# A reordered start, split products and masks on another engine in a two-layer kernel

## The chip, the cores and the metric

The kernel runs on one core of one Trainium2 chip, in one launch. The metric is the device time in microseconds (us); lower is better. The engines are TensorE (PE in the profile; its weight loads are PEld), VectorE (DVE), ScalarE (ACT), GpSimd (POOL) and SyncE (SP, which issues most DMAs). Each engine takes its instructions in the order in which they were put on its queue.

## The reference, cut to what matters

Everything is float32. The input x is (2, 1024, 512), so 2048 rows of 512. Two layers, each on a normalized copy of x:

```python
xn = _layernorm(x)
x = x + L0_attn(xn) + L0_ffn(xn)
xn = _layernorm(x)
x = x + L1_attn(xn) + L1_ffn(xn)
```

- `L0_attn` is a small branch: layer norm, a projection to 8 ranks, a linear recurrence over the 1024 rows, a projection back, and a small MLP of rank 8.
- `L0_ffn` is `fwht(silu(x @ W1.T) * (x @ W3.T)) @ W2.T` with 2048 hidden columns; `fwht` is the Walsh-Hadamard transform of the hidden row.
- `L1_attn` is causal softmax attention with 16 heads of 32, with a biased projection before it and after it.
- `L1_ffn` is `silu(x @ w_gate) * (x @ w_up)`, of each four neighbours the two largest in magnitude kept, times `w_down`.

## The kernel before, in words

**Blocks and pools.** The 2048 rows are four blocks of 512 (`TT`). `x1[i]` holds block i as four tiles of 128 rows, `xt0[i]` and `xt1[i]` hold its normalized transpose for layer 0 and layer 1. All stages are one program; three memory pools follow one another: `a` (layer 0), `b` (attention), `c` (the second feed-forward). PSUM is used as three double banks (`wide0` to `wide2`) and two single banks.

**Order.** `in_program_order` ties every instruction of PE, DVE, ACT and POOL to the one before it on its engine, in the order in which the Python code emits them. So an instruction that waits holds up everything behind it on its engine. Small work is put between the large products by hand: `put0(n, at, f, ...)` (layer 0) and `put1` (layer 1) queue a function for unit n at one of seven places, and `hook(at)` calls it there; `put0(0, 10, ...)` means unit 1, place 3.

**Gate and up products, `gate_up`, L186.** One unit is 128 columns of the hidden width for a pair of blocks (x, y). Its eight 512-wide block products are made with seven, by Winograd's scheme: `products` (L175) makes one block product, 4 matmuls, which are 8 PE records of the profile (3.43 us). The order in a unit is: `w1,x` into bank pair pa; copy to `e[0]` (L208, ACT); `s0,t0` into pc; `s1,t1` added into pa; copy to `e[1]` (L216, ACT); `other_half` into a third pair pb, added to `e[0]` on DVE (L204), then hook 3; `s2,t2` added into pa; copy to `e[2]` (L222, ACT); `e[2]` plus pc on DVE (L224); `w2,t3` added into pa; `s3,y` added into pc; `e[1]` plus pc (L234). A product that adds into pa waits until the ACT copy of pa is done; the last into pc waits until L224 has read pc. The sums `t0` to `t3` of the inputs are made by `combine_x` (L148, four DVE subtractions of 128x1024), the sums `s0` to `s3` of the weights by `combine_w` (L165, four POOL operations). Where `first` is given (unit 0 of either layer), `other_half` comes right after the copy to `e[0]`. There are 16 units in each layer: units 0 to 7 are blocks 0 and 1, units 8 to 15 blocks 2 and 3.

**The start.** `load_x` brings the tiles of block 0. `ln_stats(i, half)` makes the statistics of two tiles on DVE (L113, L114, L106) and their reciprocal deviation on POOL (L107). `ln_scale` makes the offsets on DVE (L119) and the normalized tiles z: on ACT for block 0 (L123), on DVE for block 1 (L537). `ln_turn` transposes z on PE (L132) and copies it out on ACT (L136). `ln_turn(1, 1)`, the last one, is called in `begin`, which also makes `t0` and `t1`; so the first product of the sums follows it directly. `branch_in` (L579) is 32 thin products (24 columns out) for each half of a block. `prepare` (four POOL operations) and `prepare_last` (thin products, L489 to L505) make constants of the branch.

**The transform.** The Walsh-Hadamard transform is applied to W2. `fwht_rows(q)` (L424) multiplies quarter q by a Hadamard matrix in four products, each evicted by ACT (L431); before unit 3 these use the two single banks in turn. Four `fwht_step` on DVE (L442, L443; two operations of 128x1024 each) follow, the last of them into `w2h`, from which POOL makes the sums of the down weights (L741 onward). The down products (L297) start in unit 3; the second of them waits for `hidden_first` and `hidden_last` (L265 to L273, four DVE operations).

**Attention.** The steps of `first` (row maxima) run 13 steps (`ahead`) before those of `second`, 96 steps in all, 12 for each of 8 units. A step of `second` makes scores (L1095, L1101), exponentials on ACT (L1112) into `pt`, for the diagonal block a mask on POOL (`affine_select`, L1117), then in the next step `gather` multiplies by the values (`o`, L1137) and adds `pt` into the running sum `acc` (L1145): on POOL, or on DVE once the row maxima are over. At its end stands the out-projection (`po`, L990), then layer 1's feed-forward.

**The end.** Layer 1's last group is multiplied by its down weights row block by row block (`row_down`, L1449): 4 matmuls of 512 columns, an addition on DVE (L1459), a store of 256 KB (L1462).

Of the kernel before, what the change touches and what calls it, by code (L numbers as in the profile page):

```python
# [35 lines left out]
def two_layers(ctx: ExitStack, tc: tile.TileContext, t: dict, out: bass.AP):  # L36
# [137 lines left out]

    def products(pair, a, x, start=False, stop=False):  # L175

        for m in range(2):
            for k in range(2):
                nc.tensor.matmul(  # L179
                    pair[:, m, :], a[:, m, k, :], x[:, k, :],  # L180
                    start=start and k == 0, stop=stop and k == 1, skip_group_check=True,
                )

    turns = 0

    def gate_up(pool, name, w1, w2, s, x, y, tt, h, hook, first=None):  # L186

# [12 lines left out]

        def other_half():
            pb = ps_pair(f"p1_{name}", turns % 3)
            products(pb, w1[:, :, 2:, :], x[:, 2:, :], start=True, stop=True)
            nc.vector.tensor_add(e[0], e[0], pb)  # L204
            hook(3)

# [11 lines left out]
        if not first:  # L218
            other_half()
        products(pa, s[2], tt[2])  # L220

        nc.scalar.copy(e[2], pa)  # L222
        silu(0, 0, e[0][:, 0, :])
        nc.vector.tensor_add(e[2], e[2], pc)  # L224
# [119 lines left out]
    with tc.tile_pool(name="a", bufs=1) as a:  # L344
# [78 lines left out]

        def fwht_rows(q):  # L424

            tags = ("x1_2", "x1_3") if q % 2 else ("xt_2", "xt_3")
            w2x[q] = [res.tile([P, NC, P], F32, tag=tag, name=f"w2{tag}_{q}") for tag in tags]
            for c in range(0, NC, 4):
                bank = one_bank(f"pw_{q}_{c}")
                nc.tensor.matmul(bank, had, w2h[:, q, c : c + 4, :], start=True, stop=True)  # L430
                nc.scalar.activation(  # L431
                    w2x[q][0][:, c : c + 4, :].rearrange("p c d -> p (c d)"), bank,
                    AF.Copy, scale=1.0 / math.sqrt(HID),
                )
# [83 lines left out]
        def ln_stats(i, half):  # L518
            js = slice(2 * half, 2 * half + 2)
            statistics(mv0[i][:, js], rs0[i][:, js], x1[i][:, js, :], 2, f"a{i}_{half}")  # L520

        zs = {}

        def z_tile(name, tag="z"):
            return a.tile([P, 2, D], F32, tag=tag, name=name)

        def ln_scale(i, half, tag="z"):


            js = slice(2 * half, 2 * half + 2)  # L530
            offsets(nm0[i][:, js], mv0[i][:, js], rs0[i][:, js])
            zs[i, half] = z_tile(f"z0_{i}_{half}", tag)
            for m in range(2):
                j = 2 * half + m
                d, x = zs[i, half][:, m, :], x1[i][:, j, :]
                if i == 1:
                    nc.vector.tensor_scalar(  # L537
                        d, x, mv0[i][:, j, 0:1], rs0[i][:, j : j + 1], ALU.subtract, ALU.mult
                    )
                else:  # L540
                    scaled(d, x, nm0[i], rs0[i], j)

        def ln_turn(i, half):
# [239 lines left out]
        for half in range(2):  # L783
            put0(0, 3, branch_in, 0, half)
            put0(0, (1, 2)[half], branch_in, 1, half)
        for q, n in enumerate(((0, 2), (0, 4), (1, 2), (1, 4))):
            put0(*n, fwht_rows, q)
            for m in range(4):
                n, at = (0, (4, 5, 6, 6)[m]) if q == 0 else divmod(4 * q + 3 + m, 7)
                put0(n, at, fwht_step, q, m)  # L790
        put0(0, 6, prepare)
        put0(2, 6, load_x, 2)
# [35 lines left out]

        for k in ((0, 0), (0, 1)):
            ln_stats(*k)  # L830
        ln_scale(0, 0)
        ln_turn(0, 0)
        ln_stats(1, 0)
        ln_scale(0, 1, "e2")
        ln_turn(0, 1)
        ln_stats(1, 1)
# [3 lines left out]
        def begin():  # L840
            nonlocal tt
            ln_turn(1, 1)
            tt, make_first, second = combine_x(a, xt0[0], xt0[1], "a0")
# [16 lines left out]
        for n in range(2 * NU):  # L860
# [7 lines left out]
            def hook(at):  # L868
# [11 lines left out]
                a, f"a{n}", *weights_of[n], xt0[i0], xt0.get(i0 + 1), tt,  # L880
                lambda m, i: h[:, 2 * (n % 2) + m, i, :], hook, begin if n == 0 else None,
            )
            for m in (2 * n + 4, 2 * n + 5):
# [19 lines left out]


    first_gu = {}
    with tc.tile_pool(name="b", bufs=1, reuse_waits="tile") as b:

# [15 lines left out]
            out=mask, in_=mask, compare_op=ALU.is_ge, fill=MASKED,  # L923
            base=0, pattern=[[-1, P]], channel_multiplier=1,
        )
        identb = b.tile([P, P], BF16, name="identb")
# [147 lines left out]
        def shift_rows(u, half):  # L1074
# [9 lines left out]
            nc.vector.tensor_copy(negs[u, half], px[:, :NJ].rearrange("p t c -> p (t c)"))  # L1084

        def weights(u, j, kt):

# [18 lines left out]
            for p in range(2):  # L1106
# [7 lines left out]
                )  # L1114
                if kt >= 4 * j:
                    d = pt[:, :, s : s + P]
                    nc.gpsimd.affine_select(  # L1117
# [5 lines left out]

        held, sums = {}, {}

        def gather(u, j, kt, s, pts):

            bb, hg = units[u]
            if kt == 0:
                held[u, j] = ps_bank(f"o_{u}_{j}", 0)  # L1130
                sums[u, j] = pts
            po = held[u, j]
# [8 lines left out]
            if kt:  # L1141

                eng = nc.vector if per * u + 4 * j + kt + ahead >= len(second) else nc.gpsimd
                for acc, pt in zip(sums[u, j], pts):
                    eng.tensor_add(acc[:, :, s:], acc[:, :, s:], pt[:, :, s:])  # L1145
# [6 lines left out]
        def total(u, j):  # L1152

            pw = ps_wide(f"w_{u}_{j}")[:, 0, :]
            for h in range(4):
                rows = slice(h * HD, (h + 1) * HD)
                nc.tensor.matmul(  # L1157
                    pw[rows, :], ones, sums[u, j][h // 2][:, h % 2, :],
                    start=True, stop=True, tile_position=(0, h * HD),
# [162 lines left out]
        for m in range(QT, QT + NJ):  # L1322
            rest.append((n, n + 9, project_out(m)))
        while rest or open_parts or fixed:
            one_part(n)
            what_is_fixed(n)
            n += 1
# [8 lines left out]
    with tc.tile_pool(name="c", bufs=1, reuse_waits="tile") as c_:  # L1336
# [112 lines left out]
        def row_down(n, i, j):  # L1449

            block = 2 * units[2 * n][0] + i
            bank = ps_wide(f"dr_{n}_{i}_{j}")[:, 0, :]
            for r in range(4):
                nc.tensor.matmul(  # L1454
                    bank, hs[n][:, r, i, j * P : (j + 1) * P], wd[n][:, r, :],
                    start=(r == 0), stop=(r == 3),
                )
            x = x1[block][:, j, :]
            nc.vector.tensor_add(x, x, bank)  # L1459
            if n % G == G - 1:  # L1460
                row = block * TT + j * P
                nc.sync.dma_start(out=out[row : row + P, :], in_=x)  # L1462

# [51 lines left out]

        tt, next_tt, second = None, None, None
        s_of = {}
# [4 lines left out]
        for n, (pb, g, half) in enumerate(units):  # L1522
# [12 lines left out]
            def hook(at):  # L1535
                nonlocal tt, next_tt, second
                if n == at == 0:
                    tt, *make = combine_x(c_, x, y, "c0")
                    for f in make:
                        f()  # L1540
                for f, *args in between1.pop((n, at), ()):
# [5 lines left out]
                if at == 5 and n == len(units) // 2 - 1:  # L1547
                    next_tt, first, second = combine_x(c_, xt1[2], xt1[3], "c1")
                    first()

            gate_up(
                c_, f"c{n}", gu_w.pop((n, 0)), gu_w.pop((n, 1)), s_of.pop(n), x, y, tt,
                lambda m, i: h[:, 2 * half + m, i, :], hook,
                (lambda: (y, tt)) if n == 0 else None,
            )
# [79 lines left out]
```

## Time and profile before

| | |
|---|---|
| median of 3 runs | 1847.09 us (1846.87, 1847.09, 1848.96) |
| the profiled execution, its own time | 1850.59 us |
| its span, first to last instruction | 1848.8 us |
| mean granted TensorE clock | 0.994 |
| PE busy | 1798.2 us, 97% |
| DVE, POOL, ACT busy | 1127.4 us (61%), 821.1 us (44%), 478.5 us (26%) |
| DMA | 68.12 MB, mean 37 GB/s |

A timeline line gives start, duration, engine, line of the kernel, operation, tiles and shapes, and in square brackets the idle time before it and what ended it. Lines merge neighbours of one kind; a matmul in float32 counts as two records. A line of the waits gives who waited for whom, the total in us, how often, and the longest. A line of the stretches (windows) gives the busy time and number of instructions of PE, PEld, DVE, ACT and POOL, then the granted clock (PEclk), the DMA share and GB/s. Before the first record of the clock (20.7 us) the PEclk column shows 1.00 whatever it was; there the durations tell it.

### The profile page before, as it was taken

Reading aid. Unit: us, or ns where it says so; the run is one execution under the profiler, and the core shown is the slowest. Engines: PE = TensorE matmul, PEld = TensorE weight load, DVE = VectorE, ACT = ScalarE, POOL = GpSimd, SP = SyncE. Lnnn points to the kernel's source line nnn. Section 1 sums busy time; section 2 is a strip of 40 time slices with the busy share of each in tenths; the row PEclk is TensorE's granted clock in tenths of the full one; section 3 lists DMA queues with packets and bytes.
Section 4 is the critical chain, followed back from the end, with each engine's and each line's share of the span. In section 5 each row is a group of like instructions: output and inputs, shape, how many; then the busy total and the mean of one; then the engine's idle time right before and its main releaser. Section 6 shows DMA issues by size and latency. Waiting matters only on the chain.

```text
span 1848.8 us, 18896 instructions
## 1 busy us (share of the span) xinstructions
PE 1798.2 (97%) x7348; PEld 918.6 (50%) x7348; DVE 1127.4 (61%) x1464; ACT 478.5 (26%) x683; POOL 821.1 (44%) x711
## 2 busy tenths in 40 slices
PE   6999999999999999999999999999999999999999
PEld 4446565655655564333333333333455555555544
DVE  3685444565543438565657656642768678768665
ACT  2322222122221102334333443412211221212120
POOL 4335364246552222467667756732244244343410
PEclk9999999999999999999999999999999999999999
DMA  6121111011101100000001000011101101211101
GB/s 228 35 80 34 35 35 38 31 46 35 35 23 34 35 7 23 1 12 12 13 1 35 12 12 1 24 46 34 35 23 57 57 23 58 91 35 46 46 1 46
DMA packets 29465, 68.12 MB, mean 37 GB/s; under 512 B 3392, under 2 KB 11584, under 8 KB 27840
## 3 DMA queue, kind: packets, MB, share of 16 engines
q1 hardware_dynamic: 28656, 66.61, 10.9%
q8 instruction: 59, 0.97, 0.2%
q10 hardware_dynamic: 720, 0.30, 0.1%
q14 instruction: 30, 0.25, 0.0%
HBM read 62.70 MB, written 4.19 MB: 36 GB/s over the span
## 4 chain that ended last, share of the span: by engine, by line
PE 88%; DVE 5%; POOL 2%; ACT 2%; issue 2%; DMA 1%; ACTq 0%; POOLq 0%; DVEq 0%
PE p_a L179 20%; PE p_c L179 19%; PE d L297 19%; PE pq L990 6%; PE m L1042 4%; PE s L1095 4%; PE o L1137 3%; PE po L990 3%; PE pv L990 3%; PE dr L1454 2%; POOL acc L1145 2%; PE w L1157 1%; DVE tops L1050 1%; PE pp L579 1%; PE s L1101 1%
## 5 line engine op out<-in xcount | busy, mean ns | idle before, releaser
L315 POOL TENSOR_TENSOR x<-x,de 128x512 f32<-128x512 f32 x87 | 125.9, 1462 | 298.4 <-DVE x L310 163.7
L1145 POOL TENSOR_TENSOR acc<-acc,pt 128x1024 f32<-128x1024 f32 (+3 forms) x138 | 233.7, 1719 | 0.0
L1050 DVE TENSOR_REDUCE tops<-m 128x2 f32<-128x1024 f32 (+2 forms) x192 | 180.8, 956 | 49.1 <-PE m L1042 44.7
L310 DVE TENSOR_TENSOR x<-x,d 128x512 f32<-128x512 f32 x145 | 99.3, 685 | 149.8 <-PE d L297 148.6
L1112 ACT ACTIVATE pt<-s 128x1024 f32<-128x1024 f32 (+3 forms) x160 | 115.1, 766 | 180.3 <-PE s L1101 167.1
L297 PE MATMUL d<-td,h 128*128 128x256 f32 x592 | 139.9, 380 | 2.2 <-DVE h L272 2.2
L297 PEld LDWEIGHTS d<-td,h 128*128 128x128 f32 x592 | 112.2, 190 | 46.2 <-issue 29.0
L990 PE MATMUL pq<-xt,wqk 128*128 128x512 f32 x256 | 125.1, 617 | 0.8 <-ACT qk L1006 0.8
L179 PE MATMUL p_a<-t_a,s_a 128*128 128x512 f32 x256 | 119.2, 610 | 2.1 <-DVE t_a L156 2.1
L179 PE MATMUL p_a<-xt,w 128*128 128x512 f32 x256 | 117.7, 603 | 0.7 <-ACT xt L136 0.7
L179 PE MATMUL p_c<-xt,s_c 128*128 128x512 f32 x256 | 115.2, 593 | 2.5 <-DVE e_c L224 1.4
L179 PE MATMUL p_a<-xt,s_a 128*128 128x512 f32 x256 | 116.6, 598 | 0.0
L179 PE MATMUL p_c<-xt,gu 128*128 128x512 f32 x256 | 114.9, 592 | 0.0
L179 PE MATMUL p_c<-t_c,s_c 128*128 128x512 f32 x256 | 114.6, 592 | 0.0
L1049 DVE TENSOR_TENSOR m<-m,mask 128x256 f32<-128x256 f32 x128 | 54.7, 427 | 98.2 <-PE m L1042 93.7
L1042 PE MATMUL m<-qk,qk 32*128 32x512 f32 (+3 forms) x768 | 107.7, 536 | 3.6 <-ACT acc L1112 3.0
L1095 PE MATMUL s<-qk,qk 32*128 32x512 f32 (+3 forms) x768 | 93.8, 532 | 3.7 <-ACT pt L1112 2.3
L172 POOL TENSOR_TENSOR s_c<-gu,s_c 128x512 f32<-128x512 f32 x16 | 20.4, 1275 | 135.9 <-PE p_c L179 135.9
L1117 POOL TENSOR_SCALAR_AFFINE_SELECT pt<-pt 128x256 f32<-128x256 f32 x112 | 48.4, 448 | 71.2 <-ACT pt L1112 70.6
L990 PEld LDWEIGHTS pq<-xt,wqk 128*128 128x128 f32 x256 | 44.5, 191 | 66.5 <-issue 62.1
L179 PEld LDWEIGHTS p_a<-xt,s_a 128*128 128x128 f32 x256 | 47.2, 190 | 57.1 <-issue 56.7
L179 PEld LDWEIGHTS p_c<-xt,s_c 128*128 128x128 f32 x256 | 48.5, 190 | 54.2 <-issue 52.9
(240 smaller groups left out, 3049.2 us busy)
## 6 DMA issues: line engine op xcount, KB each, us to landing
w<-in_W SPq DMA_DIRECT2D x32, 512.0 KB, 3.6
gu<-in_gu SPq DMA_DIRECT2D x32, 512.0 KB, 3.6
wd<-in_down SPq DMA_DIRECT2D x8, 1024.0 KB, 4.8
x<-in_x SPq DMA_DIRECT2D x16, 256.0 KB, 4.2
w2h<-in_W2q SPq DMA_DIRECT2D x4, 1024.0 KB, 11.7
xr<-in_x SPq DMA_DIRECT2D x16, 256.0 KB, 2.7
wqk<-in_WqkvT SPq DMA_DIRECT2D x16, 256.0 KB, 3.2
out_x<-x SPq DMA_DIRECT2D x16, 256.0 KB, 2.0
```

The source lines that it names most:

```text
L179: nc.tensor.matmul(pair[:, m, :], a[:, m, k, :], x[:, k, :], start=start and k == 0, stop=stop and k == 1, skip_group_check=True,)
L297: nc.tensor.matmul(out_[:, j, :], lhs[:, q, j * P : (j + 1) * P], rhs[:, q], start=m in (0, 1, 3, 4) and j == q == 0, stop=j == q == 1, sk ...
L310: nc.vector.tensor_add(r, r, out_)
L315: nc.gpsimd.tensor_add(r, r, u2[half])
L990: nc.tensor.matmul(got[0], lhs(k), rhs(k), start=(k == 0), stop=(k == KC - 1))
L1042: nc.tensor.matmul(pair[h // 2][:, h % 2, :e], q[rows, qt * P : (qt + 1) * P], k[rows, c * 512 : c * 512 + e], start=True, stop=True,)
L1049: nc.vector.tensor_add(d, d, mask.unsqueeze(1).to_broadcast([P, 2, P]))
L1050: nc.vector.tensor_reduce(out=tops[u][:, c, qt, 2 * p : 2 * p + 2], in_=pair[p][:, :, :e], axis=mybir.AxisListType.X, op=ALU.max,)
L1095: nc.tensor.matmul(pair[h // 2][:, h % 2, s:], k[rows, kt * P : (kt + 1) * P], q[rows, cols], start=True, stop=False,)
L1112: nc.scalar.activation(pt[:, :, s:], pair[p][:, :, s:], AF.Exp, scale=1.0 / math.sqrt(HD))
L1137: nc.tensor.matmul(po[rows, s:], v[:, rows], pts[h // 2][:, h % 2, s:], start=(kt == 0), stop=last, tile_position=(0, h * HD),)
L1145: eng.tensor_add(acc[:, :, s:], acc[:, :, s:], pt[:, :, s:])
```

## The change

1. **Start.** Before anything else PE makes 8 products of the identity with itself (`keep_awake`), then 4 and 3 with parts of x tiles 1 and 3; nobody reads their bank. The statistics of tiles 2 and 3 are split (`tile_stats`) around the scaling of the first half; the second half of block 0 is scaled on DVE, its offsets after it; all that comes ahead of block 1's statistics.
2. **Block 1's last transposes** move from `begin` to hook 3 of unit 0, between the two `branch_in` of block 0. `prepare` moves from hook 6 to hook 1 of unit 0.
3. **The transform's rows** come two products at a time, in eight hooks instead of four; the first quarter's steps come one hook later.
4. **`split`** in `gate_up`: `other_half` is cut in two, one half before `s2,t2` and one after it, with the addition L204 and hook 3 behind the second. It is used in unit 2 of layer 0 and in units 0, 1 and 14 of layer 1; unit 0 of layer 1 no longer uses `first`.
5. **Attention.** In the last unit the masks are minima with `allowed` on DVE, instead of `affine_select` on POOL; in exchange the running sums of its first half stay on POOL.
6. **Layer 1's first input sums** are made during the out-projection after attention, in a pool `sums` of their own.
7. **The very last `row_down`** goes in two column halves, each with its own addition and store.

```diff
-    def products(pair, a, x, start=False, stop=False):
+    def products(pair, a, x, start=False, stop=False, of=(0, 1)):
-        for m in range(2):
+        for m in of:
...
-        def other_half():
-            pb = ps_pair(f"p1_{name}", turns % 3)
-            products(pb, w1[:, :, 2:, :], x[:, 2:, :], start=True, stop=True)
-            nc.vector.tensor_add(e[0], e[0], pb)
-            hook(3)
+        def other_half(of=(0, 1)):
+            nonlocal pb
+            if 0 in of:
+                pb = ps_pair(f"p1_{name}", turns % 3)
+            products(pb, w1[:, :, 2:, :], x[:, 2:, :], start=True, stop=True, of=of)
+            if 1 in of:
+                nc.vector.tensor_add(e[0], e[0], pb)
+                hook(3)
...
         if not first:
-            other_half()
+            other_half((0,) if split else (0, 1))
         products(pa, s[2], tt[2])
         nc.scalar.copy(e[2], pa)
+        if split:
+            other_half((1,))
         silu(0, 0, e[0][:, 0, :])
         nc.vector.tensor_add(e[2], e[2], pc)
...
-        def fwht_rows(q):
+        def fwht_rows(q, half):
...
-            for c in range(0, NC, 4):
+            for c in range(NC // 2 * half, NC // 2 * (half + 1), 4):
...
+        def tile_stats(i, j):
+            st = sm.tile([P, 4, 6], F32, tag="st", name=f"st_a{i}_{j}")
+            nc.vector.bn_stats(st[:, 0, :], x1[i][:, j, :])
+            nc.vector.bn_aggr(mv0[i][:, j, :], st[:, 0, :])
...
             put0(0, 3, branch_in, 0, half)
+            if half == 0:
+                put0(0, 3, ln_turn, 1, 1)
             put0(0, (1, 2)[half], branch_in, 1, half)
-        for q, n in enumerate(((0, 2), (0, 4), (1, 2), (1, 4))):
-            put0(*n, fwht_rows, q)
+        for q, places in enumerate(((2, 4), (5, 6), (10, 11), (12, 13))):
+            for half, at in enumerate(places):
+                put0(0, at, fwht_rows, q, half)
             for m in range(4):
-                n, at = (0, (4, 5, 6, 6)[m]) if q == 0 else divmod(4 * q + 3 + m, 7)
-                put0(n, at, fwht_step, q, m)
-        put0(0, 6, prepare)
+                put0(0, (5, 6, 6, 7)[m] if q == 0 else 4 * q + 3 + m, fwht_step, q, m)
+        put0(0, 1, prepare)
...
-        for k in ((0, 0), (0, 1)):
-            ln_stats(*k)
+        def keep_awake(n, what):
+            bank = ps_pair(f"awake_{n}", 2)[:, 0, :P]
+            for _ in range(n):
+                nc.tensor.matmul(bank, ident, what, start=True, stop=True)
+        keep_awake(8, ident)
+        ln_stats(0, 0)
+        keep_awake(4, x1[0][:, 1, :P])
+        tile_stats(0, 2)
         ln_scale(0, 0)
+        tile_stats(0, 3)
+        rstd(rs0[0][:, 2:4], mv0[0][:, 2:4, 1], "a0_1")
+        keep_awake(3, x1[0][:, 3, :P])
         ln_turn(0, 0)
+        ln_scale(0, 1, "e2", True)
+        ln_turn(0, 1)
         ln_stats(1, 0)
-        ln_scale(0, 1, "e2")
-        ln_turn(0, 1)
         ln_stats(1, 1)
...
-                if kt >= 4 * j:
-                    d = pt[:, :, s : s + P]
+                d = pt[:, :, s : s + P]
+                if kt >= 4 * j and idle_vector(u, j, kt - 1):
+                    nc.vector.tensor_tensor(
+                        d, d, allowed.unsqueeze(1).to_broadcast([P, 2, P]), ALU.min
+                    )
+                elif kt >= 4 * j:
                     nc.gpsimd.affine_select(
...
-                eng = nc.vector if per * u + 4 * j + kt + ahead >= len(second) else nc.gpsimd
+                eng = nc.vector if j and idle_vector(u, j, kt) else nc.gpsimd
...
+        first_tt, *make = combine_x(sums, xt1[0], xt1[1], "c0")
+        for m, f in enumerate(make):
+            put(n + 5 + m, f)
...
+            count = 2 if (n, i, j) == (groups - 1, 1, 3) else 1
+            for m in range(count):
+                ds = slice(m * D // count, (m + 1) * D // count)
...
-                if n == at == 0:
-                    tt, *make = combine_x(c_, x, y, "c0")
-                    for f in make:
-                        f()
...
-                (lambda: (y, tt)) if n == 0 else None,
+                lambda m, i: h[:, 2 * half + m, i, :], hook, split=n < 2 or n == len(units) - 2,
```

## The prediction, made before the result was known

> **What bounds the kernel now.** I read the page first, then PE's waits, then the timeline around each wait, then clock and busy time by stretches.
>
> ```profile
> PE 1798.2 (97%) x7348; PEld 918.6 (50%) x7348; DVE 1127.4 (61%) x1464; ACT 478.5 (26%) x683; POOL 821.1 (44%) x711
> ```
>
> PE is busy 1798.2 of 1848.8 us, so at most about 50 us of idle time, plus what a halved clock costs, can be won. PE's waits name it:
>
> ```profile
> PE pt_a L132 <- ACT z L123: 11.1, 2, 9.2
> PE o L1137 <- POOL pt L1117: 4.0, 7, 1.8
> PE p_c L179 <- ACT e_c L222: 3.3, 3, 1.1
> ...
> PE pw L430 <- ACT w2x L431: 2.2, 2, 1.8
> ...
> PE p_a L179 <- DVE t_a L156: 2.1, 1, 2.1
> ...
> PE p_a L179 <- ACT e_a L222: 1.1, 1, 1.1
> ```
>
> Each of these lines is touched: start, masks, split, transform, start again, split. The timeline of the start:
>
> ```profile
> 8.18 0.15 DVE L119 SCALAR_TENSOR_TENSOR nm<-mv,rs 128x2 f32<-128x2 f32 x1
> 8.37 1.52 ACT L123 ACTIVATE z<-x,nm,rs 128x512 f32<-128x512 f32 x2 [3.58 <-DVE nm L119]
> ...
> 12.16 1.52 ACT L123 ACTIVATE z<-x,nm,rs 128x512 f32<-128x512 f32 x2 [0.33 <-DVE nm L119]
> ...
> 15.67 6.21 PE L179 MATMUL p_a<-xt,w 128*128 128x512 f32 x8 [0.68 <-ACT xt L136]
> ...
> 33.13 5.99 PE L179 MATMUL p_a<-t_a,s_a 128*128 128x512 f32 x8 [2.08 <-DVE t_a L156]
> ```
>
> A product (8 records) takes 3.43 us elsewhere; here two take about 6: a halved clock. The stretches show when that happens:
>
> ```profile
> 27.57:30.99 3.42, 3.13 (x27) 2.85 (x26) 0.00 (x0) 0.73 (x3) 0.00 (x0) 1.00 0.96 286
> 30.99:34.40 3.41, 1.33 (x3) 0.78 (x3) 2.57 (x4) 0.74 (x2) 0.00 (x0) 0.50 0.05 19
> 34.40:37.81 3.41, 3.41 (x5) 1.34 (x5) 0.28 (x2) 0.00 (x0) 1.02 (x1) 0.50 0.00 0
> 54.88:58.29 3.41, 1.66 (x4) 0.87 (x5) 2.69 (x4) 2.67 (x5) 0.00 (x0) 1.00 0.00 0
> ...
> 1317.81:1321.22 3.41, 1.61 (x6) 0.38 (x4) 3.41 (x4) 1.01 (x1) 1.28 (x1) 1.00 0.07 26
> 1321.22:1324.64 3.42, 3.42 (x7) 2.52 (x8) 3.32 (x5) 2.31 (x2) 0.00 (x0) 0.50 0.00 0
> ```
>
> PEclk is decided in steps of 3.41 us: 1.61 us of products in a step (1317.81) were followed by 0.50, 1.66 us (54.88) were not; a step full of thin products and transposes (27.57) was followed by 0.50. One halved step under dense products loses 1.7 us.
>
> **The change part by part** (us, against the profiled 1848.8 span; the execution took 1850.59, 1.8 outside the span and 3.5 over the median 1847.09, from which I subtract the total; the gap may be two halved steps, which I can't show).
>
> *Start.* The offsets at 8.18 wait behind the statistics of tiles 2 and 3 (DVE 6.37 to 8.27), though the deviation (POOL) is there at 7.34. With one tile ahead (0.69 + 0.18, done 7.27) ACT starts near 7.6, 0.8 earlier. The second half stands now behind block 1's statistics, which wait for DMAs until 9.67 and 10.95. New: tile 3 to 8.5, ve 0.17, POOL 0.7, two scalings on DVE 1.0 (L537 took 1.00): z at 10.5 instead of 13.68. From z to the first product took 15.67 − 13.68 = 1.99, so the product starts at 12.5: **3.2 won** (2.8 with transposes at half clock, 3.5 at full). Queued behind on DVE are block 1's statistics: its z comes near 15.1 instead of 14.9, needed at 12.5 + 3.43 = 15.9. Covered; a slow DMA would cost its lateness.
>
> The 15 unread products: 8 of 128 columns at half clock are 8 × 0.43 = 3.4, the others 1.7 and 1.3, all before z at 8.4: PE only waited there, so they cost nothing. What they win depends on the clock. The step 13.92 to 17.33 held 1.7 us of products and 1.1 of transposes, and the product went on at half speed until 20.75. Between the last unread product (8.4) and 12.5 stand only transposes, 4.1 us: a step of 3.41 falls mostly inside, so the clock, once up, is likely down again. *The Trainium skill ("TensorE: Matmul & The Clock Gate", Part 4) says that transposes do not count as PE-busy for the gate; this speaks against the unread products, and by it their gain would be nil.* By the rows: nothing to 2.6 (6.05 − 3.43); I take **0.6**, near the rows of 13.92.
>
> The last transposes: from the end of the thin products (29.67) to 33.13 pass 3.46, of which transposes 1.05. Now thin products of 1.86 lie over the two copies (1.07) and the subtraction (1.23); 0.5 remains: **1.9 won** (1.2 to 2.3). The thin stretch shrinks from 7.1 to about 5.3 us, still over a step: the clock still falls, but one halved step (1.7) is lost instead of 4.68 / 2 = 2.34: **0.6** (0 to 1.2). `prepare` on POOL comes ahead of a deviation (L107) that nobody needs before unit 2, and of unit 1's weight sums; it waits for its DMAs (issued to 23.6, 5.7 to 10.7 to landing, so until about 29) while POOL idles from 22.8: nothing.
>
> *Transform.* Four rows on two banks made PE wait for ACT (0.60 each): 54.66 to 56.63 and 93.15 to 93.55. Two per hook find the banks free, and their 1.72 still covers the copy to `e[2]` (1.01): **2.3 won** (1.8 to 2.4). Steps one hook later: DVE has idle time there.
>
> *Split, layer 1, units 0 and 1.* The idle times are 1.15, 1.10 and 1.10, with refill more: unit 0 takes 26.63 (1249.36 to 1275.99), unit 1 25.40, against 7 × 3.43 = 24.03. Half a product (1.72) covers the copy (1.01). The addition L204 (1.22) now starts after the second half, L224 (1.22) after it; both fit under `t3` (3.43). **4.0 won** (3.3 to 4.0). Without that cover 1.3 comes back each.
>
> *Split, unit 2 of layer 0.* Here hook 3 holds DVE work:
>
> ```profile
> 116.61 1.22 DVE L204 TENSOR_TENSOR e_a<-e_a,p_a 128x1024 f32<-128x1024 f32 x1 [1.40 <-PE p_a L179]
> 117.75 1.22 DVE L442 TENSOR_TENSOR w2x<-w2x 128x1024 f32<-128x1024 f32 x1
> 118.89 1.22 DVE L443 TENSOR_TENSOR w2x<-w2x 128x1024 f32<-128x1024 f32 x1
> 121.53 1.22 DVE L224 TENSOR_TENSOR e_a<-e_a,p_a 128x1024 f32<-128x1024 f32 x1 [1.43 <-ACT e_a L222]
> ```
>
> With the second half after `s2,t2`, L204 can't start before 120.05; three operations later L224 starts at 123.5, 2.0 late. PE wins 0.3 (`s3` at 124.8 instead of 125.09). But from L224 to L272 at 136.02 DVE is idle 0.7 us in all, and that 0.7 is part of the chain; the down product at 137.64 already waits 0.36 for L272. So PE arrives at 137.0 and waits to 139.6: **2.0 lost** (1.3 won if the chain has slack after all). A wait of 2.6 leaves under 1.6 of products in most steps that touch it: a halved step at about 3 in 4, **1.3 lost**.
>
> *Split, unit 14.* DVE is busy 1743.06 to 1763.5 without a pause: L204 runs at 1756.49, four `hidden` operations follow, L224 ends at 1762.2, and `s3` starts at 1762.36 after a wait of 1.39. None of this waits for pb, so `s3` can't start earlier: the 1.1 before `t3` only joins the 1.4 before `s3`, **0 won** (−0.3 to 1.3), and one wait of 2.9 halves a step at about 3 in 4: **1.3 lost**.
>
> *Masks.* Of the waits <- POOL, 4.2 lie in the last unit. DVE takes 16 masks; the nearest row, L1049 of the same shape, took 0.43. At 1185.68 (1.25) and 1190.24 (0.37) DVE has room: about 1.3 won. Further on it has not:
>
> ```profile
> 1203.40:1217.40 14.00, 11.48 (x84) 3.79 (x75) 13.53 (x14) 5.23 (x9) 8.33 (x9) 0.93 0.23 84
> ```
>
> There 8 masks (0.35 spacing, 2.8) queue between reciprocals (0.94) and additions (1.24). Following the queue, the mask of step 6 ends near 1212.8 (1.3 of it from earlier), so that `o` starts 2.1 before its 1214.77. The first half's 6 additions go back to POOL (1.8 each at 768 columns), which has until 1201.69. The halved step at 1215.41 may go too: **2.5 won** (−3 to 4).
>
> *Sums ahead.* Four subtractions of 1.22 lie between the additions L1179 that leave DVE idle 2.75 of each 3.43: nothing on PE; unit 0 had hidden them too. Loss if the shifted pool makes a tile wait for the last `po`: up to 1.6 (5.1 of weight sums on POOL less one product).
>
> *End.* Behind PE's last product stand an addition of 0.69 and a store landing 2.0 after issue; the half addition is 0.42: **0.3 won** (−0.3 to 0.6). The two `allowed` operations: nothing.
>
> Sum: 3.2 + 0.6 + 1.9 + 0.6 + 2.3 + 4.0 − 2.0 − 1.3 − 1.3 + 2.5 + 0.3 = **10.8**; 1847.1 − 10.8 = **1836.3**.
>
> **The rivals.**
> *A, DVE takes nothing back.* The splits in units 2 and 14 pay their 1.3 each and no step is halved: 4.6 + 2.6 better, 18.0, **1829.1**. For: DVE is idle half of layer 0. Against: the rows at 116.61 and the pauseless DVE of unit 14.
> *B, the masks make DVE the bound.* If each of the 8 masks delays `o` by its 0.43, 3.4 lost for 2.5 won: **1842.2**. For: 13.53 of 14.0. Against: `o` now waits for POOL, which has the division of the sums ahead of its masks.
> *C, DVE's delay from unit 2 doesn't end (slower).* If the 2.0 us go on as a wait of 1.2 in each of the 13 units 3 to 15 of layer 0, 15.6 is lost: 1847.1 − 10.8 + 15.6 = **1851.9**. It decides from 10.8 / 13 = 0.8 per unit. Against: from 139.3 to 160 DVE is busy 9.7 of 20.7.
> *D, the unread products don't do what they say*: the first product stays at half clock; contained above (0.6 only), 1836.9. If they do, 2.0 more: 1834.3.
>
> **How the numbers follow.** Main case with D 0.58, A 0.17, B 0.15, C 0.04, other mishaps 0.06. The range reaches from A to just past B: 1829.0 to 1843.0. This kernel can be told from no change by about 0.2%, 3.7 us, so faster means under 1843.4: main, A, and B with most of its spread, 0.90; within 0.2% 0.06; slower 0.04.
>
> **What would show it.** First full product near 12.5, the first of the sums near 27.5. No idle before L430. Units 0 and 1 of layer 1 take 24.1. In unit 3 the second down product waits about 2.6 for L272; in unit 14 `s3` waits about 2.9 for L224, with PEclk 0.50 behind most such waits. In the last attention unit `o` waits for DVE instead of POOL. Wrong if units 2 and 14 show no such wait, or if PE's idle time appears at a place not named here.

## The result, and the profile after

The changed kernel takes **1833.7 us** (median of 6 runs, 1833.09 to 1835.46) against 1848.31 (6 runs, 1846.87 to 1849.49): ratio **0.9924, 95% interval 0.9914 to 0.9935**. The forecast was 1836.3 in a range of 1829.0 to 1843.0. The profiled execution took 1834.55 us (span 1832.8, mean granted clock 0.995), 16.0 less than the profiled one of before, which lay 2.3 over its median.

The page's busy line and PE's waits after (who waited for whom, us in total, times, longest; line numbers are those of the changed file: L200 `up`, L210 the addition of pb, L228 the copy to `e[2]`, L232 `e[2]` plus pc, L280 `hidden`, L305 the down product, L553 scaling on DVE, L1161 the minima, L1165 POOL's mask, L1185 `o`, L1192 the running sums):

```profile
PE 1795.2 (98%) x7386; PEld 922.2 (50%) x7386; DVE 1126.8 (61%) x1477; ACT 476.8 (26%) x681; POOL 815.8 (45%) x703
```

```profile
PE d L305 <- DVE h L280: 4.3, 4, 2.5
PE o L1185 <- DVE pt L1161: 4.2, 5, 1.6
PE p_c L179 <- DVE e_c L232: 3.7, 1, 3.7
...
PE p_a L179 <- DVE e_a L232: 0.9, 1, 0.9
...
PE pt_a L132 <- ACT z L123: 0.6, 1, 0.6
```

The 11.1 us for `z` are 0.6. Most of that is not time won: 9.2 of the 11.1 was PE's wait before its first instruction, and the unread products stand in it now; the first full product starts 3.8 earlier. The waits for `w2x`, for `t_a` and for the copy to `e[2]` are gone. Three others head the list: the second down product (2.5 in one piece), `o` for the minima, and `s3` of unit 14 (3.7); the 0.9 is the wait before `s3` in unit 2 of layer 0. The timeline of the start:

```profile
7.59 1.52 ACT L123 ACTIVATE z<-x,nm,rs 128x512 f32<-128x512 f32 x2 [2.77 <-DVE nm L119]
...
9.40 1.00 DVE L553 TENSOR_SCALAR z<-x,mv,rs 128x512 f32<-128x512 f32 x2 [0.82 <-POOL rs L107]
...
11.88 3.70 PE L179 MATMUL p_a<-xt,w 128*128 128x512 f32 x8 [0.71 <-ACT xt L136]
...
24.58 3.67 PE L179 MATMUL p_a<-t_a,s_a 128*128 128x512 f32 x8
```

Not only do the first product and the first of the sums start earlier (15.67 and 33.13 before): both now run at full speed, 3.70 and 3.67 instead of 6.21 and 5.99. The two places where a wait grew, in the same view:

```profile
109.19 1.21 DVE L232 TENSOR_TENSOR e_a<-e_a,p_a 128x1024 f32<-128x1024 f32 x1
...
123.66 1.57 DVE L280 TENSOR_TENSOR h<-h 128x512 f32<-128x512 f32 x1
125.28 3.45 PE L305 MATMUL d<-td,h 128*128 128x256 f32 x8 [2.47 <-DVE h L280]
...
1743.09 1.21 DVE L232 TENSOR_TENSOR e_c<-e_c,p_c 128x1024 f32<-128x1024 f32 x1
1744.45 6.22 PE L179 MATMUL p_c<-xt,s_c 128*128 128x512 f32 x8 [3.71 <-DVE e_c L232]
```

And the stretches there, one step of the clock each (busy time and instructions of PE, PEld, DVE, ACT, POOL, then PEclk):

```profile
121.43:124.85 3.42, 1.39 (x4) 0.32 (x2) 3.28 (x3) 0.00 (x0) 3.42 (x3) 1.00 0.00 0
124.85:128.26 3.41, 2.98 (x7) 2.44 (x8) 2.02 (x2) 0.00 (x0) 1.50 (x1) 0.50 0.00 0
...
1739.36:1742.77 3.41, 1.38 (x4) 0.31 (x2) 3.31 (x6) 2.43 (x2) 0.00 (x0) 1.00 0.00 0
1742.77:1746.18 3.41, 1.73 (x2) 0.84 (x3) 3.31 (x5) 1.12 (x2) 0.00 (x0) 0.50 0.00 0
1746.18:1749.59 3.41, 3.41 (x5) 1.35 (x4) 0.11 (x1) 0.00 (x0) 0.00 (x0) 0.50 0.00 0
```

In this execution each long wait is followed by halved steps, one in unit 3 and two in unit 14.

**Where the 16.0 us come from.** I set each PE instruction of the two traces beside its counterpart and read how far after is ahead:

| up to | ahead by, us | made here |
|---|---|---|
| first full product starts | 3.8 | +3.8 |
| it ends | 6.3 | +2.5 (clock) |
| first product of the sums starts | 8.55 | +2.25 |
| it ends | 10.85 | +2.3 (clock) |
| unit 2, after the transform | 13.7 | +2.85 |
| unit 3, after its down products | 10.9 | −2.8 |
| last unit of attention begins | 12.35 | +1.45 (a halved step of before, 809 to 813, has no counterpart) |
| its end | 13.05 | +0.7 |
| units 0 and 1 of layer 1 | 17.1 | +4.0 |
| unit 2 there | 18.85 | +1.75 (a halved step of before, at 1321, has none) |
| unit 14 | 15.35 | −3.5 |
| end | 16.0 | +0.65 |

### The profile page after: what moved, and what is told of

Its sections match the earlier page's. It is cut to its first block, busy times and chain, and to the rows that moved or that the text cites. A ratio compares the mean times of both kernels' runs of the same rounds, so it can differ in the third digit from the quotient of the medians.

```text
span 1832.8 us, 18971 instructions
## 1 busy us (share of the span) xinstructions
PE 1795.2 (98%) x7386; PEld 922.2 (50%) x7386; DVE 1126.8 (61%) x1477; ACT 476.8 (26%) x681; POOL 815.8 (45%) x703
## 4 chain that ended last, share of the span: by engine, by line
PE 89%; DVE 6%; POOL 3%; ACT 2%; issue 1%; ACTq 0%; POOLq 0%; DVEq 0%
PE p_a L179 20%; PE p_c L179 20%; PE d L305 19%; PE pq L1030 6%; PE m L1082 4%; PE s L1139 4%; PE o L1185 3%; PE po L1030 3%; PE pv L1030 3%; PE dr L1508 2%; POOL acc L1192 2%; ACT acc L1156 1%; PE w L1204 1%; DVE tops L1090 1%; PE s L1145 1%
## 5 line engine op out<-in xcount | busy, mean ns | idle before, releaser
L1192 POOL TENSOR_TENSOR acc<-acc,pt 128x1024 f32<-128x1024 f32 (+3 forms) x144 | 243.3, 1716 | 0.1
L305 PE MATMUL d<-td,h 128*128 128x256 f32 x592 | 141.4, 383 | 4.3 <-DVE h L280 4.3
L305 PEld LDWEIGHTS d<-td,h 128*128 128x128 f32 x592 | 113.2, 192 | 48.7 <-issue 29.2
L1185 PE MATMUL o<-pt,v 128*32 128x512 f32 (+3 forms) x640 | 70.4, 478 | 5.5 <-DVE pt L1161 4.2
```

What stands on the lines that cost most here:

```text
L305: nc.tensor.matmul(out_[:, j, :], lhs[:, q, j * P : (j + 1) * P], rhs[:, q], start=m in (0, 1, 3, 4) and j == q == 0, stop=j == q == 1, sk ...
L1185: nc.tensor.matmul(po[rows, s:], v[:, rows], pts[h // 2][:, h % 2, s:], start=(kt == 0), stop=last, tile_position=(0, h * HD),)
```

## The experiments

Each time is a median with its range, beside the kernel before on the same chip (1848.07 for e1 to e4, 1848.79 for e5 to e8, 1848.45 for e9 and e10, 1848.44 for e11 and e12). After was timed beside 1848.31, so up to 0.5 us of a difference from after can lie in the chip. They answer four questions: did the unread products win anything, what do the splits in units 2 and 14 cost, what are the minima worth, and does a version without the losses exist.

**e1: no unread products.** After, without

```diff
-        keep_awake(8, ident)
...
-        keep_awake(4, x1[0][:, 1, :P])
...
-        keep_awake(3, x1[0][:, 3, :P])
```

> The changed kernel without its 15 unread products. Theory G (the unread products raise the clock before the first transposes, and transposes keep up a clock that is up): without them the first full product starts at half clock and takes about 6 us instead of 3.7, its start comes some 0.5 later, so 2 to 3.5 us are lost: 1836 to 1837, PEclk first recorded near 16 to 19 us. Rival D (they hardly matter, as the prediction had it, 0.6): 1834.3, no more than 1 us from the changed kernel.

Measured: 1834.87 (1833.7 to 1838.12, 5 runs), ratio 0.9932 (0.992 to 0.9945); the profiled execution took 1836.61. Its first two products of note in the timeline:

```profile
12.89 5.61 PE L179 MATMUL p_a<-xt,w 128*128 128x512 f32 x8 [0.68 <-ACT xt L136]
...
27.89 6.63 PE L179 MATMUL p_a<-t_a,s_a 128*128 128x512 f32 x8
```

The first product starts 1.0 later, since the transposes too go at half clock, and both products are slow again. On the median it is 1.2 behind after, between the two expectations; the spread of its runs overlaps.

**e8: the unread products alone, in the kernel before** (with `keep_awake` as in after):

```diff
-        for k in ((0, 0), (0, 1)):
-            ln_stats(*k)
+        keep_awake(8, ident)
+        ln_stats(0, 0)
+        keep_awake(4, x1[0][:, 1, :P])
+        ln_stats(0, 1)
+        keep_awake(3, x1[0][:, 3, :P])
```

> The kernel before with the 15 unread products alone (8, then 4 after the first statistics, 3 ahead of the first transposes), nothing moved. Theory G (transposes keep up a clock that is up, if they come densely): here the two bursts of 1 us are followed by waits of 1.8 and 0.7, so a step holds only 1 to 1.6 us of them; the clock may fall before the first product. Between 0 (fell) and 3 us (kept) faster than the kernel before: 1845 to 1848. By rival D nothing: 1847.5 to 1848.5.

Measured: 1848.23 (12 runs, 1842.46 to 1850.94), ratio 0.9991 (0.998 to 1.0002). Four of the 12 runs lie between 1842.46 and 1843.31 with mean granted clocks of 0.996 and 0.997, the other eight between 1847.01 and 1850.94 with 0.991 to 0.993. The profiled one is of the first kind, and even there the clock fell at 11.27:

```profile
7.85:11.27 3.41, 1.46 (x10) 0.84 (x8) 2.41 (x10) 2.59 (x4) 0.70 (x1) 1.00 0.97 351
11.27:14.68 3.41, 1.97 (x8) 1.57 (x8) 3.18 (x12) 2.58 (x5) 2.08 (x4) 0.50 1.03 426
```

In the start of before, `z` comes so late that a step holds 1.46 us of PE work, and what the products had raised is lost. Alone they win nothing clear of the noise on the median, although four runs lie below all 17 runs of the kernel before on that chip (lowest 1845.95). Together with the earlier `z`, e1 and e10 speak for a gain of 1.2 and 1.7, each within overlapping ranges.

**e2: no split in unit 2 of layer 0.** In layer 0's call of `gate_up`:

```diff
-                n == 2,
+                False,
```

> The changed kernel without the split in unit 2 of layer 0. Theory (the split delays L224 by three DVE operations, and the second down product of unit 3 waits for the chain behind it): the wait of 2.5 there shrinks to about 0.4, the halved clock after it goes, the idle 1.1 before t3 comes back: 2 to 3.5 us faster, 1830.2 to 1831.7. Rival A (the split pays its 1.3 and the wait in unit 3 has another cause): 1.1 to 1.3 us slower, 1835.

Measured: 1831.48 (1830.49 to 1832.29, 4 runs), ratio 0.9911 (0.9896 to 0.9926), 2.2 less than after. PE's waits between 100 and 130 us:

```profile
PE p_a L179 <- ACT e_a L228: 1.1, 1, 1.1
PE d L305 <- DVE h L280: 0.4, 1, 0.4
```

The 2.47 is 0.4 again, the 0.9 before `s3` is gone and so is the halved step, for the 1.1 that the split had covered: 1.9 less idle time, of the 2.2 on the medians. So the split loses here for the reason that the prediction gave, though 2.2 and not 3.3.

**e3: the split stays, the transform's step that stands ahead of L232 comes one hook earlier.**

```diff
-                put0(0, (5, 6, 6, 7)[m] if q == 0 else 4 * q + 3 + m, fwht_step, q, m)
+                put0(0, (5, 6, 6, 7)[m] if q == 0 else 4 * q + 3 + m - (q == 3 and m == 2), fwht_step, q, m)
```

> The changed kernel with one fwht_step (quarter 3, step 2) at hook 2 of unit 2 instead of hook 3, so that DVE does it while it waits for the split half; the split stays. Theory: L224 follows L204 at once, the wait of 0.9 before s3 and of 2.5 in unit 3 both go, and the halved clock with them: 3.5 to 4.7 us faster than the changed kernel, 1829.0 to 1830.2, and 1 to 1.5 better than without the split. Rival (it is the late second half itself, not the step between, that delays the chain): within 1 us of the changed kernel, 1833 to 1834.5.

Measured: 1832.59 (1830.25 to 1833.24, 4 runs), ratio 0.9914 (0.99 to 0.9928). The wait before `s3` is gone as expected, the one in unit 3 is not (PE's timeline):

```profile
122.98 1.99 PE L305 MATMUL d<-td,h 128*128 128x256 f32 x8 [1.36 <-DVE h L280]
```

This missed the expectation. From L232 to L280 there is a chain of DVE work nearly without a pause (106.90 to 122.93 in this trace), so a PE that comes 1.1 earlier waits 1.0 longer (1.36 against 0.36). Before that chain the split is worth nothing, even where it delays nobody: e3's median is 1.1 over that of e2, with ranges that overlap.

**e4: no split in unit 14.**

```diff
-                lambda m, i: h[:, 2 * half + m, i, :], hook, split=n < 2 or n == len(units) - 2,
+                lambda m, i: h[:, 2 * half + m, i, :], hook, split=n < 2,
```

> The changed kernel without the split in unit 14 of layer 1. Theory (DVE is busy without a pause there, s3 can't start before L224, so the split only joins two waits into one that is long enough to halve the clock): the wait of 3.7 becomes 1.1 and 1.4, the halved clock goes: 2 to 4.5 us faster, 1829.2 to 1831.7. Rival A (the split pays): 1.1 to 1.3 us slower, 1835.

Measured: 1830.27 (1829.62 to 1830.66, 4 runs), ratio 0.9903 (0.989 to 0.9917), 3.4 less than after. PE's waits between 1700 and 1800 us, and the two steps that stand in the place of the halved ones:

```profile
PE p_c L179 <- DVE e_c L232: 1.4, 1, 1.4
...
PE p_c L179 <- ACT e_c L228: 1.1, 1, 1.1
```

```profile
1739.36:1742.77 3.41, 2.01 (x6) 0.73 (x5) 3.27 (x5) 1.33 (x3) 0.00 (x0) 1.00 0.00 0
1742.77:1746.18 3.41, 3.41 (x9) 1.50 (x8) 1.54 (x3) 0.30 (x1) 0.29 (x1) 1.00 0.00 0
```

One wait of 3.71 became two of 1.1 and 1.4 with a product between them, and the clock stayed up: 1.2 less idle time, and no halved step where after has two. The two halved steps held 1.73 and 3.41 us of work, so they lose half of that, 2.6; with the 1.2 that makes 3.8, for 3.4 measured.

Why the joined wait is 3.71 and not 2.5 shows on POOL and DVE, first in after, then in e4:

```profile
1733.95 1.29 POOL L171 TENSOR_TENSOR s_c<-gu,gu 128x512 f32<-128x512 f32 x1 [1.32 <-PE p_c L179]
1734.14 1.65 DVE L1459 TENSOR_TENSOR first<-first,way 128x1024 bf16<-128x1024 bf16 x1
```

```profile
1732.71 0.69 DVE L1459 TENSOR_TENSOR first<-first,way 128x1024 bf16<-128x1024 bf16 x1
...
1735.95 1.46 POOL L171 TENSOR_TENSOR s_c<-gu,gu 128x512 f32<-128x512 f32 x1 [4.75 <-PE p_c L179]
```

With the split `s2,t2` ends half a product earlier, and POOL's L171, which starts right behind it, now runs beside DVE's L1459. That takes 0.96 longer and moves the pauseless queue up to L232 back with it. The same operation takes 1.64 or 1.65 in all six profiles with this split (after, e1, e2, e3, e5, e6) and 0.69 in all the others. The remaining 0.25 has no cause shown.

**e7: the edits of e2 and e4 at once**, so that only units 0 and 1 of layer 1 are split.

> The changed kernel with the split in units 0 and 1 of layer 1 only (neither unit 2 of layer 0 nor unit 14 of layer 1). Theory: the two losses are 700 units apart in the trace and add up, 2.2 + 3.4 = 5.6 us faster than the changed kernel: 1827.3 to 1829. Rival (one of the two was luck with halved steps): 1830 to 1831.5.

Measured: 1828.57 (1827.94 to 1830.04, 4 runs), ratio 0.989 (0.9877 to 0.9903), 5.1 less than after: the two gains add up (2.2 + 3.4 = 5.6).

**e5: masks on POOL again**, and the first half's sums on DVE, as before.

```diff
-                if kt >= 4 * j and idle_vector(u, j, kt - 1):
+                if False:
...
-                eng = nc.vector if j and idle_vector(u, j, kt) else nc.gpsimd
+                eng = nc.vector if idle_vector(u, j, kt) else nc.gpsimd
```

> The changed kernel with the masks of the last attention unit on POOL and its running sums on DVE, as before the change. Theory Q (the minima queue on DVE, so PE's waits there are 5.0 us now against 4.2 before; the trace of before lost 1.7 more to a halved step, which need not come back): 0 to 0.9 us faster than the changed kernel without a halved step, up to 1 slower with one: 1832.8 to 1834.7. The prediction's view (the minima win 2.5): 1836.2.

Measured: 1835.76 (1834.37 to 1839.48, 6 runs), ratio 0.9934 (0.9922 to 0.9946), 2.1 more than after: so the minima would win 2.1, near the prediction's 2.5, with ranges that overlap. The trace gives another account of it. From the last score product of the row maxima to the last product of `po`, PE is idle 4.86 us with POOL's masks and 5.87 with the minima. What speaks for the minima is the clock behind POOL's longest wait (1.81, before step 6 of `o`):

```profile
1200.78:1204.19 3.41, 1.60 (x22) 0.72 (x21) 3.11 (x4) 0.66 (x2) 3.41 (x4) 1.00 0.55 123
1204.19:1207.61 3.42, 3.42 (x4) 1.00 (x4) 1.52 (x3) 0.00 (x0) 0.90 (x2) 0.50 1.01 424
```

**e6: minima and the first half's sums, both on DVE.**

```diff
-                eng = nc.vector if j and idle_vector(u, j, kt) else nc.gpsimd
+                eng = nc.vector if idle_vector(u, j, kt) else nc.gpsimd
```

> The changed kernel with the running sums of the last unit's first half on DVE again, the masks staying on DVE. Theory P (the six POOL additions run beside the minima and stretch them from about 0.4 to 1.4 us each, which makes the wait of 1.3 before o): the minima there take 0.4 to 0.5, the wait goes, 0.7 to 1.7 us faster: 1832.0 to 1833.0. Rival Q (queueing on DVE: the additions then stand ahead of the minima and cost as much): 1833.3 to 1835.

Measured: 1831.55 (1829.28 to 1834.64, 4 runs), ratio 0.9906 (0.9893 to 0.9919), 2.1 less than after. The timeline of POOL and DVE around the first half's minima, first in after, then DVE's in e6:

```profile
1174.41 8.23 POOL L1192 TENSOR_TENSOR acc<-acc,pt 128x768 f32<-128x768 f32 x6
1175.81 5.56 DVE L1161 TENSOR_TENSOR pt<-pt,allowed 128x256 f32<-128x256 f32 x4 [1.17 <-ACT pt L1156]
```

```profile
1172.55 0.91 DVE L1161 TENSOR_TENSOR pt<-pt,allowed 128x256 f32<-128x256 f32 x2 [1.17 <-ACT pt L1156]
1173.46 1.83 DVE L1192 TENSOR_TENSOR acc<-acc,pt 128x768 f32<-128x768 f32 x2
1175.21 0.76 DVE L1161 TENSOR_TENSOR pt<-pt,allowed 128x256 f32<-128x256 f32 x2
1175.88 1.29 DVE L1192 TENSOR_TENSOR acc<-acc,pt 128x512 f32<-128x512 f32 x2
```

In after four minima take 5.56 us, 1.4 each, while POOL adds; without POOL at work they take 0.38 to 0.46 (0.91 and 0.76 for two), and DVE does the four minima and the sums of both steps in less time (1172.55 to 1177.17) than it needed for the minima alone. PE's idle time in this stretch falls from 5.87 to 4.99, by 0.9; the 2.1 of the medians is more than theory P's 0.7 to 1.7, and what made the rest is not shown.

**e9: the edits of e6 and e7 together**: splits in units 0 and 1 of layer 1 only, and the sums on DVE.

> The kernel after, with split only in units 0 and 1 of layer 1, and with the running sums of the last attention unit's first half on DVE again, beside its minima. Theory S (the minima were stretched by the additions that POOL had been given): what the two edits won singly adds up, 1828.6 - 2.1, so 1826.5 (1825.5 to 1827.6), and no minimum of step 1172 to 1182 lasts over 0.8 us. Rival T (what the sums won was the chance of one halved step fewer): 1828.1 to 1829, as with two splits alone.

Measured: **1827.59** (1825.97 to 1828.12, 4 runs), ratio **0.9884 (0.987 to 0.9899)**, the lowest median of all; 1.0 under e7, at the upper edge of theory S and under T. In its profile the four minima take 0.91 and 0.75 for two again, but a step in the stretch is halved (1179.7 to 1183.1), as in e6 and e10 (there two), while after and e7 have none there. So of the sums' gain over e7 the profile shows 0.9 us of idle time, and takes 1.7 back in the clock.

**e10: e9 without the unread products** (e9 with the edit of e1).

> The kernel of e9 without the 15 unread products. Theory U (the unread products are worth 1 to 4 us in the reordered start, since without them the first product and often that of the sums run at half clock): 1.2 to 4 over e9. Rival V (what e1 lost was chance): within 0.8 of e9.

Measured: 1829.27 (1826.93 to 1830.29, 4 runs), ratio 0.9893 (0.9877 to 0.991), 1.7 over e9, where e1 was 1.2 over after. Both point the same way, theory U's, with ranges that overlap.

**e11: e9 with all masks on POOL. e12: e9 with minima in the first half of the last unit alone.** In e9, for e11 and for e12:

```diff
-                if kt >= 4 * j and idle_vector(u, j, kt - 1):
+                if False:
```

```diff
-                if kt >= 4 * j and idle_vector(u, j, kt - 1):
+                if not j and kt >= 4 * j and idle_vector(u, j, kt - 1):
```

> The kernel of e9 with all masks of the last attention unit on POOL again, as before the change. From the last score product of the row maxima to the last product of the out-projection PE is idle 4.85 us with the masks on POOL (before, e5, e8), 5.87 with minima and the first half's sums on POOL (after, e7), 5.0 with minima and these sums on DVE (e6, e9). Theory W (that idle time decides): within 0.8 of e9. Theory X (what e5 lost, 2.1, is the halved step behind the 1.81 us wait before the last products of o, in nearly every run): 1.2 to 2.2 slower than e9.

> The kernel of e9 with minima in the first half of the last unit alone, and POOL's masks in its second half. By the waits of the single halves (0.42 and 0.75 with minima and sums on DVE against 1.26 and 0.37 with POOL's masks; in the second half 0.43, 0.29 and 1.81 with POOL's masks against 1.60, 0.17, 0.79 and 0.59 with minima) the idle time would be 4.3. Theory W: 0.5 to 0.7 faster than e9 and e11. Theory X: as slow as e11, since the wait of 1.81 is there too.

Measured: e11 1830.44 (1827.11 to 1834.88, 5 runs), ratio 0.99 (0.9883 to 0.9917); e12 1829.5 (1828.06 to 1833.26, 5 runs), ratio 0.99 (0.9883 to 0.9918). PE's idle time in the stretch came out as worked out, 4.83 and 4.38 against 5.03 in e9; yet they are 2.9 and 1.9 slower, so idle time does not decide. The step behind the 1.81 is halved in both (from 1198.4 and from 1199.0). That is theory X, but only half shown: e11's 2.9 is beyond its 2.2, e9's profiled execution lost a halved step in the same stretch, and in the profiles of e11 (24.2, 1300.8) and e12 (1301.4) others are halved elsewhere. Of the five profiles with this wait of 1.81, four have the halved step behind it (before, e5, e11, e12) and e8 has none; of the nine with minima there, whose longest wait is 1.6, none has one. Three pairs (e5 with after, e11 and e12 with e9) put masks on POOL in the second half 1.9 to 2.9 behind, with ranges that overlap. How much of that is the wait and how much the number of halved steps elsewhere stays open.

## Why the prediction was right, point by point

The time lies in the stated range and the waits came where they were forecast, but the terms missed in both directions by up to 3.6 us, so that their sum came this near is partly luck. No run takes out the earlier `z`, the transform's eight hooks, the split of units 0 and 1 of layer 1 or the halved last group; their gains are read from the two traces alone.

**Start: 3.2 for the earlier z.** Measured 3.8 at the start of the first product (11.88 for 12.5). z starts at 7.59 as worked out; the transposes behind it at full clock are the rest.

**The clock at the start: 0.6 and 0.6. This is the term that was mis-sized most.** The profiled executions differ by 2.5 and 2.3 there. The prediction took the value near the row at 13.92, where a step with 1.7 us of products and 1.1 of transposes had not raised the clock, and concluded that a step with transposes alone would let it fall. Two runs show the opposite. In e3 the step 8.07 to 11.48 holds nothing but 16 transposes (the last unread product ended at 7.7), and the clock stayed up:

```profile
8.07:11.48 3.41, 2.40 (x16) 1.67 (x16) 2.49 (x9) 2.94 (x6) 0.70 (x1) 1.00 0.91 329
11.48:14.90 3.42, 3.04 (x7) 1.44 (x8) 3.25 (x10) 0.33 (x1) 1.44 (x2) 1.00 1.03 424
```

In e10, where PE did nothing at all before 8.45, transposes alone raised it; the recorded rise is at 11.41, and the product that follows takes 3.70:

```profile
8.00:11.41 3.41, 2.96 (x14) 2.59 (x15) 2.49 (x9) 2.29 (x5) 0.70 (x1) 1.00 0.97 360
11.41:14.83 3.42, 2.75 (x10) 1.31 (x9) 3.25 (x10) 1.10 (x2) 1.36 (x2) 1.00 1.02 426
```

The statement of the Trainium skill that the prediction weighed ("TensorE: Matmul & The Clock Gate", Part 4: transposes do not count as PE-busy for the gate) does not hold for the transposes of this kernel. The page speaks of PE's transpose mode; here they stand in the profile as ordinary MATMUL records that take 1.08 us for 8, where the last unread products take 0.91 for 6, and whether they run in that mode no run shows. Rival D's own "if they do", 2.0 more and 1834.3, is near where the time fell. The row at 13.92 was read for the wrong thing: it shows a clock that is down and stays down after 2.73 us of work, which doesn't tell what keeps up a clock that is up. Over the runs: with the unread products and the earlier z, the first product took 3.70 in all ten profiled executions (after, e2 to e7, e9, e11, e12), and the product of the sums 3.67 in seven of them, 5.04 to 5.79 in three (e4, e5, e11). The gain of 2.3 there is thus a matter of chance. So on medians the unread products are worth 1.2 and 1.7 (e1, e10), more than the 0.6 written for them, but the 4.8 of the one pair of profiles is not theirs alone: without them, in e10, the first product took 3.70 too.

**Last transposes: 1.9; transform: 2.3.** 2.25 and 2.85. The wait for `t_a` and all idle time before the transform's rows are gone. The first product of the sums, forecast near 27.5, started at 24.58: these 2.25, the 2.5 of the clock and the 3.8 add up to its lead.

**Unit 2: −2.0 and −1.3.** −2.8 in the traces, −2.2 on the medians of e2, with the wait (2.47 for 2.6), its chain and its halved step as written. The chain, not the order in hook 3, sets it: e3. The halved step is chance: it follows the same wait in after and e1, and not in e4, e5 and e6, so 3 in 4 was too much.

**Unit 14: 0 and −1.3.** The wait came out at 3.71 where 2.9 was written (1.1 and 1.4 make 2.5). The prediction took L232's time as fixed; the split itself moved it back by 0.96, through POOL's L171 beside DVE's L1459 (e4). And it halved two steps where one was written: −3.5 in the traces, −3.4 on the medians. Here too the count is chance: two in after, e2 and e3, one in e5, none in e1 and e6. The joining of the waits was right, the size not.

**Units 0 and 1 of layer 1: 4.0.** 4.0: no wait is left in them.

**Masks: 2.5.** Its parts went otherwise: PE's idle time grew by 1.0. In the first half, where 1.3 was to be won, the sums given to POOL in exchange stretch the minima (1.4 for 0.42), which the prediction had priced at 0.35 to 0.43 from rows without POOL beside them; without that (e6) the waits are 0.42 and 0.75 against 1.26 and 0.37 with POOL's masks (e5), so 0.46 is won. In the second half `o` of step 6 was to start 2.1 earlier and came 0.14 earlier against the start of the unit (a lead of 12.49 on before, where the unit began with 12.35). The waits there are 1.60, 0.17, 0.79 and 0.59 for DVE, against 0.43, 0.29 and 1.81 for POOL before, 0.6 more in all. The longest stands behind DVE's queue:

```profile
1195.00 2.35 DVE L1192 TENSOR_TENSOR acc<-acc,pt 128x1024 f32<-128x1024 f32 x2
1197.27 0.94 DVE L1214 RECIPROCAL inv<-inv 128x128 f32<-128x128 f32 x1
1198.13 0.69 DVE L1161 TENSOR_TENSOR pt<-pt,allowed 128x256 f32<-128x256 f32 x2
```

```profile
1198.54 1.17 PE L1185 MATMUL o<-pt,v 128*32 128x384 f32 x8 [1.60 <-DVE pt L1161]
```

The 0.59, before `po` for DVE's L1226, is idle time at a place that the prediction had not named, one of its signs of being wrong. The halved step at 1215.41 that "may go too" did go: +0.7 in the traces. The medians of e5 say 2.1, of which the traces explain 0.7. So the mechanism written for this term failed; what the traces show of a gain came by the clock.

**End: 0.3.** 0.65.

**The rivals.** A (nothing lost in units 2 and 14) is refuted by e2 and e4. B (1842.2) named the right engine, but PE lost 1.0 of idle time there, where B had 3.4. C (a wait of 1.2 in each of units 3 to 15) did not happen: after lists no other wait for L280 over 0.84. The main sum was 10.8; the traces give 16.0, with 3.6 of the difference in the clock at the start, 3.2 in before's halved steps at 809 and 1321 that the sum did not hold (chance: e8, whose code there is that of before, has neither), −2.2 in unit 14 and −1.8 at the masks; the rest is 2.4 of small terms (z, last transposes, transform, unit 2, end). The profiled execution of before lay 2.3 over its median and that of after 0.85, so on medians 14.6 of the 16.0 remain.

## What to carry to other kernels

Where PE is 97% busy and a longer pause often halves its clock too, price a wait with the halved steps that may follow it, and do not join two short waits into one: 1.1 and 1.4 with a product between them cost no clock in any of the eight profiles with them, one of 3.7 cost up to two steps. A split product helps where the consumer has slack (units 0 and 1 of layer 1, 4.0 us); ahead of an engine whose queue runs without a pause it only moves the wait, and what stands on that queue is the first thing to read. When work is exchanged between DVE and POOL, take the price of an operation from rows in which the other engine is at work.

## What the runs showed of the hardware

- **The clock's steps of 3.41 us run free.** The first rise fell at 5.38 in after, 4.35 in e12 and 7.34 in e4, whose start is the same. So the same program meets them differently, and a halved step (up to 1.7 us) comes or goes with no change of the code. The thin stretch shows it, in e4 and in after:

```profile
21.00:24.41 3.41, 3.20 (x29) 2.92 (x29) 1.43 (x2) 1.27 (x3) 1.87 (x2) 1.00 1.02 420
24.41:27.82 3.41, 3.41 (x7) 1.72 (x7) 1.63 (x5) 0.20 (x1) 0.00 (x0) 0.50 1.02 378
```

```profile
22.45:25.86 3.41, 3.20 (x20) 2.49 (x20) 2.58 (x4) 0.92 (x3) 0.45 (x1) 1.00 1.02 381
25.86:29.27 3.41, 3.41 (x18) 2.13 (x16) 0.28 (x2) 0.00 (x0) 0.00 (x0) 1.00 0.83 298
```

  With the same 3.20 us of busy time, 29 instructions, nearly all thin, were followed by 0.50, and 20, with part of a full product among them, were not.
- **Busy time alone is not the rule.** A step with 1.44 us of full products (e1, from 1743.90) was not followed by a halved one; steps with 1.46 (e8), 1.60 (e5) and even 3.20 thin ones were. A clock that is down stayed down after 1.97 (e8) and 2.73 (before) and rose after 2.96 (e10). What exactly is counted stays open.
- **DVE's operations on two tiles are held up while POOL adds.** In after each of the four minima ends 0.28 us after one of POOL's additions (additions end at 1176.31, 1178.26, 1179.68, 1181.09; minima at 1176.59, 1178.54, 1179.96, 1181.37), so one minimum passes between two additions. The Trainium skill ("SBUF — State Buffer", section "SBUF: two separate sides") says that the two engines share a pair of ports under an exclusive lock, for a DVE operation with two inputs in SBUF; the rows agree. The `hidden` operations show it too: 1.57 to 1.76 beside a busy POOL (120.13 to 126.90 in after), 0.69 with POOL at rest (e4, 1737.93 to 1740.79). So does L1459 in bf16: 1.65 and 0.69 (e4).
